# Accumulating transfers for the outer sums, early stored combinations, and two more third-level pairs in a Strassen-style kernel

## The chip, the cores and the metric

The kernel runs on one core of a Trainium2 chip. The metric is device time in microseconds for one execution. A core has five engines that run their own instruction streams in the order written: TensorE (PE, matrix products), VectorE (DVE), ScalarE (ACT), GpSimd (POOL) and SyncE (SP, which here only issues transfers). Transfers (DMA) between the memory outside (HBM) and the on-chip SBUF are issued by SP, by ACT or by POOL. PE writes its results to eight banks of PSUM, from which DVE or ACT take them.

## The reference

Two layers on x of shape (32, 128, 2048), all float32:

```python
# layer 0: a mixed 1x1 convolution, then a linear layer with 16 low-rank updates
out = einsum('boi,bih->boh', agg_w, x) + agg_b[:, :, None]
out = einsum('bsd,od->bso', out, W) + bias + sum_e w_e * (out @ A_e.T) @ Bf_e.T
x = x + out
# layer 1: a grouped convolution (9 taps) with a context term, then 16 heads of FFN
out = conv(x, weight, groups=4) + ctx + bias
t = out[:, perm].reshape(b * l, 16, 128)
t = gelu(t @ up[h]) @ down[h]            # per head, 128 -> 512 -> 128
x = x + t.reshape(...)[:, unperm]
```

The kernel folds the low-rank updates into W, multiplies x by that matrix (4096 rows by 2048 by 2048, the work that the change touches), and mixes the channels afterwards.

## The kernel before

**Outer level.** The large product is split in 2 by 2 blocks and computed by a scheme of seven products (Strassen-Winograd): `ROUNDS = P1, P2, P6, P7, P5, P3, P4`. Each round runs over eight groups g of rows, so there are 56 steps (r, g), in this order; below, P2/4 is round P2, group 4. A round needs a combination of the weight blocks (`outer_weights`, loaded and combined by POOL during the round before) and each step one of the x blocks (`x_loads`, `x_combine`, L285 to L318). The 2 by 2 blocks of the result are sums of these products. They are kept in memory: a step loads the old sum (`olds_load`, L1039, by the table `ADDED`, L323), adds to it, and stores it under a new name (`part_store`, on SP's queue). p1, u1, u2, u3 are intermediate sums, c00 to c11 the results; P5 loads and stores two.

**Inner levels.** In a step, `multiply` (L333) applies the seven products again: four matrix instructions of 512 columns each. `multiply_third` (L426) takes two consecutive steps (a pair, g even and g + 1) and replaces two of the seven products of each by a third level over both: the even step has five products, the odd step five products and seven "quarters" of 256 columns, into further banks. `THIRD` lists the rounds that do so, `SKIP` (L52) the pairs (round, g // 2) that don't. The sums of a pair are stored after its odd step. After each product, DVE adds its bank to the accumulator in SBUF (L342, L435, L458); only P1, which has no old sum, writes a block first by an ACT copy (L344). A product that continues a bank waits until the bank has been read.

**POOL.** In step i, ahead of its products, POOL combines x for step i + 1 (L283 and L311 to L314), makes the third level's inputs (`third_inputs`, L417 to L420, for even g over 0 except in P6) and weights (`third_weights`, L393 to L396, at g = 0), the next round's outer weights (`combine`, L522) and, at g = 7, its inner weights (`inner_weights`, L245). P6 stores one x combination, s2 (for P3), and one of the weights, t2 (for P4), both through POOL's queue.

**Order.** The program is written with a manual schedule: every engine, and so every queue of transfers, runs its instructions in the order in which the Python code emits them. Buffers are 24 slots of 1 MB; a load into a slot waits for what used it last. In the last round (P4) the steps of the second stage (mixing, convolution) come in between products, and after it the FFN (L813 to L840).

## Time and profile before

| what | value |
|---|---|
| time, median of 3 runs | 2601.73 us (2601.64 to 2603.4) |
| time of the profiled execution | 2603.33 us |
| its span in the profile | 2601.6 us |
| PE busy | 2582.1 us (99%) |
| DVE, POOL, ACT busy | 1476.3, 1322.5, 533.6 us |
| bytes moved | 608.28 MB, 234 GB/s on average |
| the seven rounds of the large product | 49.8 to 1478 us of the span |
| even step, odd step, step without a third level | 17.17, 29.25, 24.03 us (rounds P2 to P3) |

The steps' times come from the starts of PE's instructions, in order. In a row of a timeline the columns are the start and the length in us, engine, line, operation, what is written from what, how many are merged, and the idle time before it with its releaser. In a row of waits they are who waited for whom, then the total in us, how often, and the longest. In a row of stretches, each engine's busy time and number of instructions, the granted clock, the busy share of the transfer engines and what they moved in GB/s. A suffix q (SPq, ACTq) is the engine's instruction stream as an issuer of transfers.

### The profile page before, as it was taken

The page shows a single profiled execution, that of the slowest core. Times are in us where ns is not written, and L with a number is a line of the kernel's source. Part 1 is how long each engine was busy: PE and PEld are TensorE (multiplying, and loading weights), DVE is VectorE, ACT ScalarE, POOL GpSimd, SP SyncE. Part 2 cuts the span into 40 slices and gives each one's busy share as a digit, 9 for nine tenths or more (in the row PEclk, how much of TensorE's full clock was granted, in tenths as well). Part 3 has the DMA queues.
Part 4 walks back from the last instruction along what each step waited for, and adds up shares of the span by engine and source line. Part 5 has one row for each costly group of instructions (what it writes and reads, how often), then busy time and mean ns, then how long its engine had stood idle before and what let it go on. Part 6 is the DMA issues. An engine that isn't in the chain of part 4 may idle for free. (4 is left out here: it accounts for less than half of the span.)

```text
span 2601.6 us, 21348 instructions
## 1 busy us (share of the span) xinstructions
PE 2582.1 (99%) x6876; PEld 1304.0 (50%) x6876; DVE 1476.3 (57%) x2326; ACT 533.6 (21%) x1099; POOL 1322.5 (51%) x1092
## 2 busy tenths in 40 slices
PE   9999999999999999999999999999999999999998
PEld 4444455455455555555454544555545555455543
DVE  5554465356455676544276666667666666666610
ACT  0000000000000000000011244444444444444432
POOL 7321657888986854967323234343444334434232
PEclk9999999999999999999999999999999999999999
DMA  7542458688557487474767797877777877787532
GB/s 311 221 162 99 188 194 331 262 335 324 209 227 290 185 322 299 194 311 162 249 214 259 227 308 260 254 235 226 226 235 236 257 234 222 224 253 236 166 117 89
DMA packets 188160, 608.28 MB, mean 234 GB/s; under 512 B 17680, under 2 KB 92944, under 8 KB 144016
## 3 DMA queue, kind: packets, MB, share of 16 engines
q1 hardware_dynamic: 149936, 473.74, 51.3%
q0 software_dynamic: 32704, 130.04, 14.9%
q10 hardware_dynamic: 5408, 3.13, 0.4%
q8 instruction: 55, 0.90, 0.1%
q14 instruction: 57, 0.47, 0.1%
HBM read 372.45 MB, written 200.84 MB: 220 GB/s over the span
## 5 line engine op out<-in xcount | busy, mean ns | idle before, releaser
L818 PE MATMUL bank<-t,ws 128*128 128x512 f32 x1024 | 460.4, 592 | 0.0
L829 PE MATMUL bank<-gl,ws 128*128 128x512 f32 x1024 | 460.2, 592 | 0.0
L836 POOL DMA_INDIRECT out<-t,orow x128 | 151.0, 1180 | 543.8 <-DVE t L834 482.2
L821 ACT ACTIVATE gl<-bank 128x512 f32<-128x512 f32 x512 | 306.5, 599 | 445.2 <-PE bank L818 435.4
L829 PEld LDWEIGHTS bank<-gl,ws 128*128 128x128 f32 x1024 | 194.6, 190 | 233.0 <-issue 231.0
L818 PEld LDWEIGHTS bank<-t,ws 128*128 128x128 f32 x1024 | 194.5, 190 | 226.9 <-issue 223.0
L567 POOL TENSOR_TENSOR x<-x,fb 128x512 f32<-128x512 f32 x128 | 176.4, 1407 | 224.8 <-DMA x<-in_x 153.8
L834 DVE TENSOR_TENSOR t<-bank,t 128x512 f32<-128x512 f32 x128 | 88.5, 691 | 320.4 <-PE bank L829 320.4
L573 ACT ACTIVATE bank<-w,aggb 128x512 f32<-128x512 f32 x128 | 81.0, 684 | 872.9 <-DMA w<-w_d 855.6
L439 PE MATMUL bank<-P_t,s_P 128*128 128x512 f32 x544 | 241.8, 592 | 0.0
L435 DVE TENSOR_TENSOR u<-bank,u 128x512 f32<-128x512 f32 x168 | 110.7, 688 | 196.2 <-PE bank L439 178.1
L283 POOL TENSOR_TENSOR xt<-xt,xt 128x512 f32<-128x512 f32 x128 | 161.9, 1297 | 106.1 <-DMA xt<-in_xT 88.2
L311 POOL TENSOR_TENSOR s_P<-xt 128x512 f32<-128x512 f32 x56 | 73.3, 1308 | 254.9 <-DMA xt<-in_xT 185.2
L439 PE MATMUL bank<-wo_P,s_P 128*128 128x512 f32 x448 | 199.1, 592 | 0.0
L546 DVE SCALAR_TENSOR_TENSOR ags<-mix,att_bc,ags 128x128 f32<-128x128 f32 x224 | 184.8, 825 | 4.7
L439 PEld LDWEIGHTS bank<-P_t,s_P 128*128 128x128 f32 x544 | 103.4, 190 | 115.6 <-issue 112.4
L802 POOL DMA_INDIRECT t<-hx_d,row x128 | 131.8, 1030 | 53.1 <-issue 25.1
L349 PE MATMUL bank<-P_t,s_P 128*128 128x512 f32 x352 | 154.7, 592 | 0.0
L439 PEld LDWEIGHTS bank<-wo_P,s_P 128*128 128x128 f32 x448 | 85.1, 190 | 95.2 <-issue 92.6
L674 PE MATMUL bank<-va,tw_l 128*128 128x256 f32 x512 | 122.0, 380 | 1.0 <-DVE va L658 1.0
L342 DVE TENSOR_TENSOR u<-bank,u 128x512 f32<-128x512 f32 x84 | 56.4, 685 | 110.0 <-PE bank L349 108.6
L674 PEld LDWEIGHTS bank<-va,tw_l 128*128 128x128 f32 x512 | 96.8, 190 | 43.1 <-issue 32.4
(188 smaller groups left out, 3591.5 us busy)
## 6 DMA issues: line engine op xcount, KB each, us to landing
xt<-in_xT SPq DMA_DIRECT2D x88, 1024.0 KB
u<-u_d SPq DMA_DIRECT2D x40, 1024.0 KB
wo_P<-wb_d SPq DMA_DIRECT2D x36, 1024.0 KB
u<-c_d SPq DMA_DIRECT2D x64, 512.0 KB
x<-in_x SPq DMA_DIRECT2D x32, 1024.0 KB
xg<-x SPq DMA_DIRECT2D x256, 128.0 KB
hx_d<-x1t SPq DMA_DIRECT2D x32, 1024.0 KB
hx_d<-ht SPq DMA_DIRECT2D x32, 1024.0 KB
```

What stands on the lines that cost most here:

```text
L283: nc.gpsimd.tensor_tensor(out[:, i, j], a[:, i, j], b[:, i, j], op)
L349: nc.tensor.matmul(ps, lhsT=lhs[k][:, bass.ts(kc, P)], rhs=rhs[k][kc], start=first and kc == 0, stop=last and kc == 3, skip_group_check=True,)
L435: nc.vector.tensor_tensor(acc[:, si, oi], ps, acc[:, si, oi], ALU.add)
L439: nc.tensor.matmul(ps, lhsT=lhs[k][:, bass.ts(kc, P)], rhs=rhs[k][kc], start=first and kc == 0, stop=last and kc == 3, skip_group_check=True,)
L546: nc.vector.scalar_tensor_tensor(ag, mix[:, k], att, ag, ALU.mult, ALU.add)
L567: nc.gpsimd.tensor_tensor(xt[:, f], xt[:, f], late["fb"][:, f], ALU.add)
L674: nc.tensor.matmul(out, lhsT=w[:, 2 * i + r], rhs=rhs, start=first and r == 0, stop=last and r == 1, skip_group_check=True,)
L802: nc.gpsimd.indirect_dma_start(out=t.rearrange("p k t -> p (k t)"), out_offset=None, in_=hx_d[g].rearrange("l k t -> l (k t)"), in_offset= ...
L818: nc.tensor.matmul(pu, lhsT=w[:, m * P : (m + 1) * P], rhs=t[:, 0], start=True, stop=True)
L821: nc.scalar.activation(gl[m], pu, AF.Gelu)
L829: nc.tensor.matmul(pd, lhsT=w[:, (MC + m) * P : (MC + m + 1) * P], rhs=gl[m], start=(m == 0), stop=(m == MC - 1),)
L836: nc.gpsimd.indirect_dma_start(out=out, out_offset=bass.IndirectOffsetOnAxis(ap=orow[:, g, h : h + 1], axis=0), in_=t[:, 1], in_offset=None,)
```

## The change

1. `SKIP` loses (P2, 3) and (P5, 3): steps 6 and 7 of these rounds run as a pair with the third level.
2. The sums of outer products are no longer loaded and stored under new names. A table `SUMS` gives, for each round, what it loads, where it stores, and with what operation. P1 stores its product to c00 and c01. P2, P6, P5, P3 and P4 start a fresh accumulator and add it to the sums in memory by an accumulating transfer issued by POOL. P7 alone loads a sum (c01, which is then P1 + P6), adds to it and stores it to c11 and c10. The stores of a step are issued at its end (for a pair after the odd step). With a fresh accumulator the first write of each block is an ACT copy.
3. Combinations for later rounds are stored where they first arise: x(1,0) + x(1,1) for P5 in round P6 (s1), x(0,0) - x(1,0) for P7 in round P1 for g > 1 (s3; one more load, four POOL additions and a store on POOL's queue), and the weights of P7 at the combination for P6 (t3). P7 (g > 1) and P5 then load one x block, P7's weights one block for each kc.
4. s1, s2, t2 and t3 are stored through ACT's queue; s2 and t2 were on POOL's.

```diff
-SKIP = (("P2", 3), ("P6", 3), ("P5", 3))
+SKIP = (("P6", 3),)
...
-            "P7": lambda: [x_load(g, 0, 0), x_load(g, 1, 0)],
-            "P5": lambda: [x_load(g, 1, 0), x_load(g, 1, 1)],
+            "P7": lambda: [part_load("s3", g)] if g > 1 else [x_load(g, 0, 0), x_load(g, 1, 0)],
+            "P5": lambda: [part_load("s1", g)],
...
-            b, a, c = ts
-            pieces(b, b, a, ALU.add)
-            pieces(a, b, c, ALU.subtract)
-            part_store("s2", g, a)
-        if r in ("P7", "P5", "P3"):
-            pieces(a, a, ts[1], ALU.add if r == "P5" else ALU.subtract)
+            b, c, a = ts
+            pieces(b, b, c, ALU.add)
+            part_store("s1", g, b, nc.scalar)
+            pieces(a, b, a, ALU.subtract)
+            part_store("s2", g, a, nc.scalar)
+        elif len(ts) > 1:
+            pieces(a, a, ts[1], ALU.subtract)
...
+    SUMS = {
+        "P1": (None, ("c00", "c01"), None),
+        "P2": (None, ("c00",), ALU.add),
+        "P6": (None, ("c01",), ALU.add),
+        "P7": ("c01", ("c11", "c10"), None),
+        "P5": (None, ("c01", "c11"), ALU.add),
+        "P3": (None, ("c01",), ALU.add),
+        "P4": (None, ("c10",), ALU.add),
     }
+    def sum_store(r, g, acc):
+        for n in SUMS[r][1]:
+            if SUMS[r][2]:
+                nc.gpsimd.dma_start(
+                    part_d[n, g], acc.rearrange("p k s c -> p (k s c)"), accum_op=SUMS[r][2]
+                )
+            else:
+                part_store(n, g, acc, nc.sync)
+
+    def put(acc, fresh, si, oi, ps):
+        to = acc[:, si, oi]
+        if (si, oi) in fresh:
+            nc.vector.tensor_tensor(to, ps, to, ALU.add)
+        else:
+            nc.scalar.copy(to, ps)
+            fresh.update([(si, oi), (si, oi, 0), (si, oi, 1)])
+
+    def begin(r, g, old):
+        if old is not None:
+            return old, {(si, oi, *h) for si in range(2) for oi in range(2) for h in ((), (0,), (1,))}
+        return slot(f"m_{r}{g}", (P, 2, 2, QW)), set()
...
         def combine():
+            def keep(d, t):
+                nc.scalar.dma_start(d[kc], t.rearrange("p k o c -> p (k o c)"))
+
             if len(ts) > 1:
                 pieces(ts[0], ts[0], ts[1], ALU.subtract)
             if len(ts) > 2:
-                pieces(ts[0], ts[0], ts[2], ALU.add)
-                nc.gpsimd.dma_start(t2_d[kc], ts[0].rearrange("p k o c -> p (k o c)"))
-            return ts[0]
+                keep(t3_d, ts[0])
+                pieces(ts[2], ts[0], ts[2], ALU.add)
+                keep(t2_d, ts[2])
+            return ts[-1 if len(ts) > 2 else 0]
...
+    def sum_begin(i):
+        sums[i] = begin(*steps[i], olds.pop(i))
...
+        if ri == 0 and g > 1:
+            other = x_load(g, 1, 0)
         if in_pair(r, g):
...
+        if ri == 0 and g > 1:
+
+            pieces(other, xa[i], other, ALU.subtract)
+            part_store("s3", g, other)
         xa.pop(i - 1, None)
         if in_pair(r, g) and g % 2 == 0 and (g == 0 or r == "P6"):
             sq = third_inputs(i, nc.vector)
+        for what in stores:
+            sum_store(*what)
+        stores.clear()
```

More of the change, by code (lines that the diff above doesn't have):

```diff
@@ L104, in adaln_ffn_kernel @@
     t2_d = {kc: scratch(f"t2_d{kc}") for kc in range(4)}
+    t3_d = {kc: scratch(f"t3_d{kc}") for kc in range(4)}
     w1_d = scratch("w1_d", (1, L))
@@ L111, in adaln_ffn_kernel @@
         (n, g): scratch(f"{n}_d{g}")
-        for n in ("s2", "p1", "u1", "u2", "u3", "c00", "c01", "c10", "c11")
+        for n in ("s1", "s2", "s3", "c00", "c01", "c10", "c11")
         for g in range(NG)
@@ L320, in adaln_ffn_kernel, with multiply @@
     xa = {}
-    ADDED = {
-        "P1": [(None, "p1")],
-        "P2": [("p1", "c00")],
-        "P6": [("p1", "u1")],
-        "P7": [("u1", "u2")],
-        "P5": [("u1", "u3"), ("u2", "c11")],
-        "P4": [("u2", "c10")],
-        "P3": [("u3", "c01")],
-    }
-    def multiply(r, g, lhs, rhs, olds, between):
+    SUMS = {
[6 more added lines that the diff above has]
+        "P4": (None, ("c10",), ALU.add),
+    }
+    def sum_store(r, g, acc):
[17 more added lines that the diff above has]
+        return slot(f"m_{r}{g}", (P, 2, 2, QW)), set()
+    def multiply(r, g, lhs, rhs, acc, between):
         px, py, pz = bank(), bank(), bank()
-        accs = olds if olds[0] is not None else [slot(f"m_{r}{g}", (P, 2, 2, QW))]
-        fresh = set()
+        acc, fresh = acc
         def add(si, oi, ps):
-            for acc in accs:
-                to = acc[:, si, oi]
-                if olds[0] is not None or (si, oi) in fresh:
-                    nc.vector.tensor_tensor(to, ps, to, ALU.add)
-                else:
-                    nc.scalar.copy(to, ps)
-            fresh.add((si, oi))
+            put(acc, fresh, si, oi, ps)
         def product(k, ps, first, last):
@@ L376, in multiply @@
         done(px)
-        for (_, new), acc in zip(ADDED[r], accs):
-            part_store(new, g, acc, nc.sync)
+        stores.append((r, g, acc))
     def third_weights(name, rhs):
@@ L424, in third_inputs, with multiply_third @@
         }
-    def multiply_third(r, g, lhs, rhs, olds, between, quarters, sq):
+    def multiply_third(r, g, lhs, rhs, acc, between, quarters, sq):
         px, py = bank(), bank()
+        acc, fresh = acc
         if sq:
             qx, qy, qz = bank(), bank(), bank()
-            both = [held.pop(), olds]
+            both = [held.pop(), (acc, fresh)]
         def add(si, oi, ps):
-            for acc in olds:
-                nc.vector.tensor_tensor(acc[:, si, oi], ps, acc[:, si, oi], ALU.add)
+            put(acc, fresh, si, oi, ps)
         def product(k, ps, first, last):
@@ L455, in quarter @@
             for b, h in to:
-                for acc in both[b]:
-                    part = acc[:, :, 0, h * NQ : (h + 1) * NQ]
+                acc, fresh = both[b]
+                part = acc[:, :, 0, h * NQ : (h + 1) * NQ]
+                new = [si for si in range(2) if (si, 0, h) not in fresh]
+                if not new:
                     nc.vector.tensor_tensor(
@@ L460, in quarter @@
                     )
+                    continue
+                for si, p in enumerate(halves(ps)):
+                    if si in new:
+                        nc.scalar.copy(part[:, si], p)
+                        fresh.add((si, 0, h))
+                    else:
+                        nc.vector.tensor_tensor(part[:, si], p, part[:, si], ALU.add)
+                if {(1, 0, 0), (1, 0, 1)} <= fresh:
+                    fresh.add((1, 0))
         product("P1", px, True, False)
@@ L494, in multiply_third @@
         if not sq:
-            held.append(olds)
+            held.append((acc, fresh))
             return
-        for b, accs in enumerate(both):
-            for (_, new), acc in zip(ADDED[r], accs):
-                part_store(new, g - 1 + b, acc, nc.sync)
-    held = []
+        for b, (acc, _) in enumerate(both):
+            stores.append((r, g - 1 + b, acc))
+    held, stores = [], []
     def outer_weights(r, kc):
@@ L514, in outer_weights @@
             "P6": [w(1, 1), w(0, 1), w(0, 0)],
-            "P7": [w(1, 1), w(0, 1)],
+            "P7": [t3_d[kc]],
             "P5": [w(0, 1), w(0, 0)],
@@ L1033, in adaln_ffn_kernel @@
     unsummed, unsummed_first = [], list(first)
-    olds = {}
+    olds, sums = {}, {}
     chain = small()
@@ L1040, in olds_load @@
         r, g = steps[i]
-        olds[i] = [old and part_load(old, g) for old, _ in ADDED[r]]
+        olds[i] = SUMS[r][0] and part_load(SUMS[r][0], g)
+    def sum_begin(i):
+        sums[i] = begin(*steps[i], olds.pop(i))
     for i, (r, g) in enumerate(steps):
@@ L1045, in adaln_ffn_kernel @@
         last_round = ri + 1 == len(ROUNDS)
+        if i == 0:
+            olds_load(0)
+        sum_begin(i)
         if i + 1 < len(steps):
@@ L1054, in adaln_ffn_kernel @@
                     sq = third_inputs(i, nc.gpsimd)
-        if i == 0:
-            olds_load(0)
         if i + 1 < len(steps) and not last_round:
@@ L1127, in between @@
                     stage(k0 + j // 2, stage_second)
+        if ri == 0 and g > 1:
+            other = x_load(g, 1, 0)
         if in_pair(r, g):
             multiply_third(
-                r, g, lhs.pop(i), rhs, olds.pop(i), between, quarters, sq if g % 2 else None
+                r, g, lhs.pop(i), rhs, sums.pop(i), between, quarters, sq if g % 2 else None
             )
         else:
-            multiply(r, g, lhs.pop(i), rhs, olds.pop(i), between)
+            multiply(r, g, lhs.pop(i), rhs, sums.pop(i), between)
+        if ri == 0 and g > 1:
+            pieces(other, xa[i], other, ALU.subtract)
+            part_store("s3", g, other)
         xa.pop(i - 1, None)
```

## The prediction

> **What bounds the kernel now.** I read the page's engine table first, then what TensorE waited for, then the stretches of single steps.

> ```profile
> PE 2582.1 (99%) x6876; PEld 1304.0 (50%) x6876; DVE 1476.3 (57%) x2326; ACT 533.6 (21%) x1099; POOL 1322.5 (51%) x1092
> ...
> PE bank L223 <- DVE w L226: 3.2, 3, 2.5
> ...
> PE bank L450 <- POOL P_q L394: 1.4, 1, 1.4
> ```

> TensorE (PE) is busy 2582.1 of 2601.6 us and no single wait is over 2.5 us. So the time is PE's own work, and anything that makes PE stand is added in full. Adding up PE's gaps between 50 and 1478 us, the seven rounds, gives 4.6 us (1.44 of them in step P6/1, where the quarter weights of L394 come late). The change can remove only matmul time or these 4.6 us; earlier loads, fewer bytes and idler engines buy nothing.

> **Part 1: two more pairs with the third level.** The stretches show what a pair (two steps) takes with it and without it, in rounds P2 and P6:

> ```profile
> core 0: us, PE busy (x) PEld busy (x) DVE busy (x) ACT busy (x) POOL busy (x), PEclk, DMA share, GB/s
> 399.36:445.78 46.42, 46.42 (x137) 25.84 (x136) 24.08 (x35) 0.00 (x0) 32.98 (x28) 1.00 0.87 331
> 445.78:493.85 48.07, 48.07 (x114) 21.28 (x113) 14.44 (x23) 0.00 (x0) 36.79 (x32) 1.00 0.70 264
> ...
> 588.39:634.81 46.42, 46.42 (x137) 25.84 (x136) 30.14 (x39) 0.00 (x0) 38.31 (x32) 1.00 0.81 304
> 634.81:682.88 48.07, 48.07 (x114) 21.28 (x113) 18.11 (x23) 0.00 (x0) 44.27 (x37) 1.00 0.66 258
> ```

> 48.07 - 46.42 = 1.65 us a pair; (P2, 3) and (P5, 3) make **-3.3 us**, all of it on PE. With PE's 4.6 us of gaps, -7.9 us is the most that this change can bring.

> **Part 2: who issues the sums.** 48 loads of old sums leave SP's queue (56 become 8) and 32 of its 64 stores; 48 accumulating transfers come to POOL's queue, at the end of a plain step or of a pair. SP's relief is worth 0 by the above. On POOL the transfer's issue is short; the nearest row is POOL's own 1 MB store at 0.573 us (L277). The trace has no accumulating transfer: below I bound its issue by 0.57 and by 1.18 us, the indirect store of L836, and take 0.57. What counts is its wait. It must wait for the last DVE add of the step, and POOL does nothing behind it meanwhile, as POOL and SP do today in the like place:

> ```profile
> POOL out L836 <- DVE t L834: 482.2, 93, 10.1
> ...
> SPq L277 <- DVE u L458: 180.2, 12, 33.2
> ```

> The first row is POOL standing before a store until DVE has the data. Queued behind the new wait is POOL's next step: the combination of the next step's x, the third-level inputs (L417 to L420), the weights of the next round. Today POOL does these ahead. For step P2/4, which PE starts at 399.36:

> ```profile
> 387.65 1.26 POOL L311 TENSOR_TENSOR s_P<-xt 128x512 f32<-128x512 f32 x1 [5.78 <-DMA xt<-in_xT]
> ...
> 392.72 1.26 POOL L417 TENSOR_TENSOR sq<-xt 128x512 f32<-128x512 f32 x1
> ...
> 397.85 9.90 POOL L283 TENSOR_TENSOR wo_P<-wo_P,wo_P 128x512 f32<-128x512 f32 x8
> 408.04 0.57 POOL L527 DMA_DIRECT2D t_d<-wo_P  x1 [0.30 <-POOL wo_P L283]
> ```

> It began 11.7 us before the step and needs 20.1 us (387.65 to 407.75). After the change the step before it is the end of a pair: PE ends at E, the two last DVE adds take until E+1.5 (today 399.56 plus 1.29), then 0.1 and the issue of 0.57: POOL begins at E+2.15. By itself that is harmless: the result of the x combination is due at E+17 and is there at E+7.3.

> **Part 3: the early stores on ACT.** This is where it hurts. Six of the seven rounds now start their sums afresh, so the first write of each block of the accumulator is an ACT copy instead of a DVE add (0.587 us by the row L344 ACT COPY m_P, where a DVE add is 0.69; ACT has room). But ACT also receives the stores of combinations (s1, s2, t3, t2; 24 x 0.33 us by today's ACTq rows of L548, some 8 us), and these stand in ACT's stream **ahead of the copies of the running step**: x_combine(i+1) and combine() come before multiply(i) in the loop. Each store waits for POOL; every copy behind it waits too; and PE waits for the copy, because product P1's bank px is added into again by product P6:

> ```profile
> 399.36 3.60 PE L439 MATMUL bank<-w,xt 128*128 128x512 f32 x8
> 402.79 7.03 PE L439 MATMUL bank<-P_t,s_P 128*128 128x512 f32 x16
> 409.66 7.03 PE L439 MATMUL bank<-w,s_P 128*128 128x512 f32 x16
> ```

> These are the five products of an even step, 3.43 us each: P1 into px, P5 into py, then P6 into px. PE arrives at P6 6.87 us into the step. In an odd step the quarters lie between and it arrives at 3.43 + 3.45 + 3.43 + 3.45 = 13.8 us.

> Round P2, steps 4 and 6 (even, with a combine()): POOL has t2 at E+2.15+20.1 = E+22.25; 0.3 to ACT's issue (as before L527's), 0.33 for it, 0.69 for the copy with its hand-over: px is free at E+23.55. PE stands 23.55 - 6.87 = 16.7 us, twice: **+33.4 us**. Steps 3, 5 and 7 are odd: POOL has gone straight on from the even step (no sum is stored there), and its store comes about 11, 4 and 0 us into the step, before 13.8: nothing.

> Round P6, every x_combine stores s1 and s2, s2 after eight additions of 1.24 us (9.9 us by the 8-fold rows of L283). Steps 0, 2, 4 (even) and 6 (plain, behind a pair; PE reaches P6 after P1 and P2, also 6.87): E + 2.15 + 9.9 + 0.3 + 0.33 + 0.69 = 13.4, less 6.87 = 6.5 us, four times: **+26.0 us**. Odd steps: s2 comes some 4 us into them, nothing; P6/7 makes P7's x, which stores nothing. Behind these lies one unknown: the three x loads of a P6 step can land after E+2.15 (today POOL waited for them up to 5.3 us in this round). From 0 to 5 us each: I take 1, **+4 us**, since most of those loads were there. Step P6/1's own gap of 1.44 us goes, as its quarter weights get the time of the stall: **-1.4**.

> Rounds P7, P5, P3, P4 store nothing on ACT that waits for POOL. P5's four transfers put POOL at E+3.4, with 10.3 us of work due at E+17; P3: 10.2 us for the next x, then 10 more due at the odd step's quarters. P7 stores through SP as today. In P1 the added x load, four POOL subtractions (5 us) and the s3 store meet a POOL that idles 20 to 30 us a step; its loads compete for buffers: 0 to 10 us, taken as 0.

> DVE loses the second sum of P5, POOL 32 + 16 additions (P5's x, P7's weights, some 60 us): off the path, and hidden by PE. POOL's additions would only count in P6, where its 44.27 us in a plain pair of 48.07 are tightest, and there x keeps all its additions.

> [...] How long does an accumulating MB occupy queue and buffer? The row: POOL's plain stores landed in 9.4 us (s_d) to 10.0 us (t_d). [...] At today's 304 to 331 GB/s loads and stores clearly overlap; P5 loses 8 MB of plain old-sum traffic and two x loads per pair and gains four adds[...]. I take the row, and no loss from it.

> **The sum.** 33.4 + 26.0 + 4 - 3.3 - 1.4 = +58.7 us on a span of 2601.6. The profiled execution took 2603.3, the three timed runs have a median of 2601.7; the same addition to the median gives **2660 us**, +2.3%.

> **Rivals.**
> - No stall (6%): ACT's stores do not hold up its copies, or POOL isn't held at the pair's end. The point that decides: t2 issued before 6.2 us of step P2/4. For it: POOL is 12 us ahead today. Against it: 20 us of POOL work now stands behind a wait for the pair's end. Then 2601.7 - 3.3 = 2598 us, down to 2594 with all gaps gone: not slower.
> - Only P2 stalls (9%): in P6 POOL gets in ahead of the copies, say because the copies are due later than I read. 2601.7 + 33.4 - 3.3 = 2632 us.
> - The adds are slow (10%): accumulating transfers take over 40 us per MB, so that their buffers and the loads behind them come late and odd steps stall too, say 5 us in each of eight further pairs: 2700 us. For it: the DMA share is already 0.87 in a P2 pair. Against it: the bytes do not grow.

> **How the numbers follow.** The forecast has 75%; with buffer waits of P1, an issue of 1.18 instead of 0.57 (six stalls, up to two issues each: +7) and loads 0 to 5 us late in P6, it spans 2645 to 2685. To leave out no more than 2 in 10 the range takes in the second rival and the lower part of the third: 2632 to 2690. A change within 0.2%, 5.2 us, can't be told from none here: the first rival gives 4% same and 2% faster, the rest is slower, 94%.

> **What would show it.** Right: PE gaps of about 17 us in P2/4 and P2/6 and of 6 to 7 us in P6/0, 2, 4, 6, each ended by the ACT copy into the accumulator; ACT standing behind POOL's combinations; pairs P2/6-7 and P5/6-7 shorter by 1.65 us apart from gaps; SP's store waits shrunk. Wrong: PE still 99% busy, PE gaps ended by loads, or gaps in P5 and P3.

## The result, and the profile after

| | before | after |
|---|---|---|
| time, median | 2602.57 us (4 runs, 2601.64 to 2603.75) | 2707.12 us (4 runs, 2704.47 to 2709.5) |
| ratio, 95% interval | | 1.0401 [1.0389, 1.0414] |
| profiled span | 2601.6 us | 2707.7 us |
| bytes moved | 608.28 MB | 581.01 MB |

The changed kernel is 4.0% slower: +106.1 us of span, where +58.7 was forecast. Fewer bytes and fewer loads bought nothing, and TensorE (PE) is where the time went. The profile's engine row and its row of granted clock, in 40 slices of 67.7 us, read:

```profile
PE 2601.4 (96%) x6924; PEld 1321.3 (49%) x6924; DVE 1400.2 (52%) x2120; ACT 627.4 (23%) x1274; POOL 1315.0 (49%) x1094
...
PEclk9999898899899999999999989999999999999999
```

PE's share fell from 99 to 96%, and its busy time *rose* by 19.3 us with only 48 more matmuls. The second row says why: five slices show a clock below nine tenths (slices 5, 7, 8, 11 and 24 of 40), and each of them holds a stretch in which PE had stood. What it stood for, by the view of waits:

```profile
PE bank L457 <- ACT m_P L351: 51.8, 5, 16.8
PE bank L368 <- ACT m_P L351: 22.6, 2, 16.0
PE bank L850 <- DMA t<-hx_d,row: 10.7, 1, 10.7
PE bank L457 <- POOL s_P L313: 6.9, 1, 6.9
```

The matmuls of the three kinds of step are now L368, L457 and L468, the DVE add of `put` is L349, its ACT copy L351, the accumulating transfer L339, the FFN's gather L834. Seven gaps end with the ACT copy that frees a PSUM bank, one with a POOL instruction that ends beside such a copy, one with the FFN's first gather. In order of time: P1/7 16.02, P2/3 5.21, P2/4 16.80, P2/6 16.72, P6/0, 2, 4 and 6 6.44, 6.59, 6.88 and 6.60, the start of the FFN 10.65 us. Nothing stands in P7, P5 or P3.

Stretches show step P2/4, the odd step P2/5 behind it, P6/0, P1/7 and pair P5/6-7 (columns as in the stretches of before):

```profile
core 0: us, PE busy (x) PEld busy (x) DVE busy (x) ACT busy (x) POOL busy (x), PEclk, DMA share, GB/s
427.46:463.64 36.18, 19.38 (x42) 8.31 (x40) 9.78 (x11) 1.66 (x3) 34.16 (x28) 0.76 0.86 301
463.64:492.89 29.25, 29.25 (x97) 18.25 (x96) 8.46 (x17) 3.09 (x6) 2.26 (x3) 1.00 0.55 154
558.00:583.48 25.48, 19.04 (x41) 8.17 (x40) 16.15 (x7) 1.66 (x3) 23.38 (x22) 0.87 0.96 329
284.09:326.76 42.67, 26.65 (x57) 11.51 (x56) 10.32 (x14) 2.34 (x4) 28.60 (x25) 0.80 0.39 151
1106.00:1152.42 46.42, 46.42 (x137) 25.86 (x136) 15.22 (x20) 4.74 (x9) 43.38 (x36) 1.00 0.63 167
```

An even step takes 17.17 us undisturbed. P2/4 takes 36.18: 17.17, the gap of 16.80, and 2.21 more, in which PE ran the step's matmuls at half the clock. The odd step behind it is whole again. The last row is the gain: 46.42 instead of 48.07.

**Where 106 us went.** Each step's length, less its undisturbed length, less its gap, is taken as what the slow clock cost: 2.63 (P1/7), 2.64, 2.21, 1.96 (P2), 1.87, 1.72, 3.21, 2.41 (P6), together 18.65, and about 2.8 at the FFN's start (5.66 us of PE time at half clock).

| term | us |
|---|---|
| six gaps that the prediction placed (P2/4, P2/6, P6/0, 2, 4, 6) | +60.0 |
| gaps that it did not place: P1/7 16.0, FFN 10.7, P2/3 5.2 | +31.9 |
| half clock behind nine gaps, 18.65 + 2.8 | +21.5 |
| third level in two pairs | -3.3 |
| small gaps of before that are gone, by the steps' lengths (-1.4 was forecast) | -4.5 |
| the rounds begin later | +1.6 |
| sum (measured: +106.1; the FFN behind its gap is 1.1 shorter than before) | +107.2 |

**The foreseen mechanism** stands in four timelines of the changed kernel, DVE's, POOL's, ACT's and PE's, around step P2/4 (columns as before):

```profile
427.66 1.29 DVE L349 TENSOR_TENSOR m_P<-bank,m_P 128x512 f32<-128x512 f32 x2 [3.01 <-PE bank L457]
```

```profile
429.25 0.86 POOL L339 DMA_DIRECT2D c_d<-m_P  x1 [8.09 <-DVE ags L576]
429.82 1.57 POOL L313 TENSOR_TENSOR s_P<-xt 128x512 f32<-128x512 f32 x1
...
440.29 9.79 POOL L284 TENSOR_TENSOR wo_P<-wo_P,wo_P 128x512 f32<-128x512 f32 x8
```

```profile
445.24 5.20 ACTq L552 DMA_DIRECT2D t_d<-wo_P  x2
450.56 1.07 ACT L351 COPY m_P<-bank 128x512 f32<-128x512 f32 x2 [24.46 <-POOL wo_P L284]
```

```profile
427.46 3.60 PE L457 MATMUL bank<-w,xt 128*128 128x512 f32 x8
430.89 3.60 PE L457 MATMUL bank<-P_t,s_P 128*128 128x512 f32 x8
451.29 5.65 PE L457 MATMUL bank<-P_t,s_P 128*128 128x512 f32 x8 [16.80 <-ACT m_P L351]
```

The pair's last adds end at 428.95. POOL issued the sum 0.30 us later (its row names a short DVE instruction of the mixing, L576, that ends in between) and began the next step's work at 429.82, 2.36 us into P2/4, where before it was 11.7 us ahead of it. Its eight weight additions end at 450.08, ACT issues t2 (the second of two merged issues) and only then copies the banks, and PE has stood for 16.80 us. Its next eight matmuls took 5.65 us instead of 3.60: the half clock.

### The profile page after: what moved, and what is told of

The parts are those of the page before. It is cut to its first block, busy times and chain, and to the rows that moved or that the text cites. A ratio compares the mean times of both kernels' runs of the same rounds, so it can differ in the third digit from the quotient of the medians.

```text
span 2707.7 us, 21413 instructions
## 1 busy us (share of the span) xinstructions
PE 2601.4 (96%) x6924; PEld 1321.3 (49%) x6924; DVE 1400.2 (52%) x2120; ACT 627.4 (23%) x1274; POOL 1315.0 (49%) x1094
## 2 busy tenths in 40 slices
DMA packets 184415, 581.01 MB, mean 215 GB/s; under 512 B 17264, under 2 KB 92528, under 8 KB 143600
## 5 line engine op out<-in xcount | busy, mean ns | idle before, releaser
L850 PE MATMUL bank<-t,ws 128*128 128x512 f32 x1024 | 463.2, 595 | 10.7 <-DMA t<-hx_d,row 10.7
L351 ACT COPY m_P<-bank 128x512 f32<-128x512 f32 x177 | 102.8, 585 | 1198.8 <-PE bank L457 447.5
L457 PE MATMUL bank<-P_t,s_P 128*128 128x512 f32 x608 | 283.7, 615 | 58.6 <-ACT m_P L351 51.8
L349 DVE TENSOR_TENSOR m_P<-bank,m_P 128x512 f32<-128x512 f32 x129 | 87.8, 690 | 480.5 <-PE bank L457 228.9
L339 POOL DMA_DIRECT2D c_d<-m_P x48 | 42.0, 933 | 386.1 <-DVE m_P L478 160.5
L457 PEld LDWEIGHTS bank<-P_t,s_P 128*128 128x128 f32 x608 | 119.8, 198 | 196.9 <-issue 173.5
L457 PE MATMUL bank<-wo_P,s_P 128*128 128x512 f32 x480 | 213.3, 592 | 0.0
L578 DVE SCALAR_TENSOR_TENSOR ags<-mix,att_bc,ags 128x128 f32<-128x128 f32 x224 | 210.0, 938 | 5.5
L834 POOL DMA_INDIRECT t<-hx_d,row x128 | 132.3, 1034 | 48.0 <-issue 25.3
L368 PE MATMUL bank<-P_t,s_P 128*128 128x512 f32 x288 | 131.2, 610 | 22.6 <-ACT m_P L351 22.6
L457 PEld LDWEIGHTS bank<-wo_P,s_P 128*128 128x128 f32 x480 | 91.3, 190 | 102.2 <-issue 99.4
L313 POOL TENSOR_TENSOR s_P<-xt 128x512 f32<-128x512 f32 x42 | 57.6, 1371 | 168.8 <-DMA xt<-in_xT 140.0
L478 DVE TENSOR_TENSOR m_P<-bank,m_P 128x512 f32<-128x512 f32 x75 | 51.8, 690 | 156.4 <-PE bank L468 155.7
L284 POOL TENSOR_TENSOR xt<-xt,xt 128x512 f32<-128x512 f32 x96 | 125.8, 1451 | 0.0
## 6 DMA issues: line engine op xcount, KB each, us to landing
c_d<-m_P POOLq DMA_DIRECT2D x48, 1024.0 KB, 10.8
```

Of the source, the lines that this page charges most:

```text
L284: nc.gpsimd.tensor_tensor(out[:, i, j], a[:, i, j], b[:, i, j], op)
L368: nc.tensor.matmul(ps, lhsT=lhs[k][:, bass.ts(kc, P)], rhs=rhs[k][kc], start=first and kc == 0, stop=last and kc == 3, skip_group_check=True,)
L457: nc.tensor.matmul(ps, lhsT=lhs[k][:, bass.ts(kc, P)], rhs=rhs[k][kc], start=first and kc == 0, stop=last and kc == 3, skip_group_check=True,)
L578: nc.vector.scalar_tensor_tensor(ag, mix[:, k], att, ag, ALU.mult, ALU.add)
L834: nc.gpsimd.indirect_dma_start(out=t.rearrange("p k t -> p (k t)"), out_offset=None, in_=hx_d[g].rearrange("l k t -> l (k t)"), in_offset= ...
L850: nc.tensor.matmul(pu, lhsT=w[:, m * P : (m + 1) * P], rhs=t[:, 0], start=True, stop=True)
```

## The experiments

Every ratio is to the kernel before, timed beside it, with its 95% interval.

**1. Early stores on POOL's queue instead of ACT's.**

```diff
-            part_store("s1", g, b, nc.scalar)
+            part_store("s1", g, b)
...
-            part_store("s2", g, a, nc.scalar)
+            part_store("s2", g, a)
...
-                nc.scalar.dma_start(d[kc], t.rearrange("p k o c -> p (k o c)"))
+                nc.gpsimd.dma_start(d[kc], t.rearrange("p k o c -> p (k o c)"))
```

> The changed kernel with the four early stores (s1, s2, t3, t2) issued by POOL instead of ACT; nothing else. Theory A (the stores stand in ACT's stream ahead of the copies, and PE waits for the copies): the seven gaps of P2/3, P2/4, P2/6, P6/0, P6/2, P6/4 and P6/6 go, 65.2 us, and with them the half clock behind each, some 16 us: about 2626 us; the gaps of P1/7 (16 us) and at the start of the FFN (10.7 us) stay. Theory B (the accumulating transfers burden memory or buffers, and the copies only show it): the transfers are all still there, so the gaps stay and the time is within 15 us of 2707.

Measured: 2640.7 us, 1.015 [1.0133, 1.0167]. PE's waits in this kernel:

```profile
PE bank L368 <- ACT m_P L351: 16.0, 1, 16.0
PE bank L850 <- DMA t<-hx_d,row: 10.8, 1, 10.8
PE bank L457 <- POOL xt L284: 5.9, 1, 5.9
...
PE bank L457 <- POOL P_t L253: 2.1, 1, 2.1
...
PE bank L468 <- POOL P_q L412: 1.1, 1, 1.1
```

All seven gaps of P2 and P6 are gone, with the same accumulating transfers and the same bytes: the stores' place on ACT is their cause, not the memory. P1/7 and the FFN, where no ACT store stands ahead of the copy, are unmoved. Most of what is left over the expectation is new: gaps of 2.08 us in P6/0 and of 5.89 and 1.14 us in P6/1. There POOL has the last step's x with the third level's inputs and P6's outer weights (20 us), P6's first x (15 us) and its inner weights (21 us): 56 us in a pair of 46.4, begun late. In the changed kernel the stalls of P2 seem to have given it that time.

**2. First writes on DVE instead of ACT.**

```diff
-            nc.scalar.copy(to, ps)
+            nc.vector.tensor_copy(to, ps)
...
-                        nc.scalar.copy(part[:, si], p)
+                        nc.vector.tensor_copy(part[:, si], p)
```

> The changed kernel with the first writes of the accumulators as DVE copies instead of ACT copies; the early stores stay on ACT. Theory A: nothing that PE waits for stands behind ACT's stores any more, so P2 and P6 lose the same gaps as with the stores on POOL, about 2626 us, though a buffer that is still being stored (P1/7, perhaps P2/3) holds a DVE copy as it held an ACT copy. Theory B: 2690 us or more. A third possibility, that DVE is then too late for PE: gaps of 1 us or less in many steps, 2640 us.

Measured: 2696.43 us, 1.0368 [1.035, 1.0385]. The number is the one of theory B, but experiment 1 speaks against that theory, and the gaps did not stay where they were. They moved: P2/5 15.16, P2/7 10.49, P6's even steps and P6/6 3.2 to 4.2, P1/7 16.19, the FFN 20.06. In P2/5, ACT's queue and DVE show why:

```profile
452.02 5.20 ACTq L552 DMA_DIRECT2D t_d<-wo_P  x2
```

```profile
437.15 0.68 DVE L351 COPY m_P<-bank 128x512 f32<-128x512 f32 x1
459.97 0.69 DVE L351 COPY m_P<-bank 128x512 f32<-128x512 f32 x1 [22.14 <-issue]
```

The copy at 459.97 is the first write into a fresh accumulator. DVE stood for 22 us until then, though nothing is in front of the copy in its stream: by the reading that experiment 12 tests in P2/3, the accumulator takes the buffer of t3, whose store ACT issued only at 452.02 and whose last packet ended at 459.44. So a late store held a copy in two ways here, by its place in ACT's stream and by the buffer it reads, and the second followed the copy from ACT to DVE. P6's smaller gaps have another cause (last section). Why the FFN's gap doubled is left open.

**3. The accumulating transfers of P2 to P3 issued in the next step, behind POOL's work for it.**

```diff
+        for what in late_sums:
+            sum_store(*what)
+        late_sums.clear()
         if ri == 0 and g > 1:
             other = x_load(g, 1, 0)
...
-            sum_store(*what)
+            if last_round or not SUMS[what[0]][2]:
+                sum_store(*what)
+            else:
+                late_sums.append(what)
```

> The changed kernel with each accumulating transfer of rounds P2 to P3 issued one step later in POOL's stream, behind POOL's preparation for the next step and ahead of that step's products; the early stores stay on ACT. Theory A (POOL is held at the end of a pair, so that its preparation and the store behind it are late): POOL works ahead again, the gaps of P2/4, P2/6 and P6/0, 2, 4, 6 shrink from 60 us to under 10 us, about 2630 to 2640 us. If ACT's stores alone were enough to hold PE, without POOL being held: the gaps stay above 40 us, 2680 us or more.

Measured: 2675.68 us, 1.0287 [1.0269, 1.0304], between the two expectations. The gaps of P2/3, P2/4 and P6/2, 4, 6 are gone and P2/6's is 0.89: that POOL was held at the pair's end is the other half of the cause. But P2/5 now has 6.78, P6/0 21.12 and P6/1 7.46. At P6/0, POOL's timeline and ACT's:

```profile
542.82 4.92 POOL L284 TENSOR_TENSOR xt<-xt,xt 128x512 f32<-128x512 f32 x4 [7.40 <-DMA xt<-in_xT]
```

```profile
535.45 12.68 ACTq L278 DMA_DIRECT2D s_d<-xt  x2
548.23 1.07 ACT L351 COPY m_P<-bank 128x512 f32<-128x512 f32 x2 [29.91 <-POOL xt L284]
```

The x load lands late and POOL waits for it, s2 stands in ACT's queue for POOL, the copy behind s2. That the deferred sums kept the load's buffer is the likely reason; it was not isolated.

**4. The third level alone: the kernel before with one line of the change.**

```diff
-SKIP = (("P2", 3), ("P6", 3), ("P5", 3))
+SKIP = (("P6", 3),)
```

> The kernel before with the third level in the pairs (P2, 3) and (P5, 3) too, and nothing else of the change. If the gain of a pair is 1.65 us and buffers suffice: 3.3 us faster, 2598 us. If POOL or the buffers are too late at the ends of these rounds: the gain is lost to new gaps in P2/6, P2/7, P6/0, P5/7 or P3/0, 2600 us or more.

Measured: 2600.23 us (12 runs) against 2602.01 (15 runs), 0.9993 [0.9984, 1.0002]. P4/7 ends at 1473.88 instead of 1478.43 us, so the rounds are 4.55 us shorter, but the median gains only 1.8. None of the gaps that were feared in these rounds is there. Part of the gain is given back later, where the FFN waits 0.5 us for its weights; the rest is not explained. This is the best version of the study, not to be told from the kernel before.

**5. The FFN's first gathers issued ahead of the last accumulating transfers.**

```diff
+        if last_round and g == 7:
+            final = list(stores)
+            stores.clear()
         for what in stores:
...
             gather_two(0)
+            for what in final:
+                sum_store(*what)
```

> The changed kernel with one edit: in the last step the FFN's first two gathers are issued by POOL ahead of the last accumulating transfer. If that transfer's wait is what makes them late: the gap at the FFN's start goes, 10.7 us and some 3 us of half clock, 2693 to 2695 us. If the gathers wait for something else (the rows they read, the buffers): 2705 us or more.

Measured: 2697.2 us, 1.0369 [1.0352, 1.0387], 9.9 us less than the changed kernel. The gap of 10.65 is gone; 2.26 us for the FFN's weights come up behind it, by which the saving falls short. In the changed kernel POOL's timeline was

```profile
1573.10 0.88 POOL L339 DMA_DIRECT2D c_d<-m_P  x1 [21.63 <-ACT m_P L351]
1574.29 1.05 POOL L834 DMA_INDIRECT t<-hx_d,row  x1 [0.30 <-issue]
```

and in the kernel before

```profile
1460.49 1.01 POOL L802 DMA_INDIRECT t<-hx_d,row  x1 [4.71 <-DVE x L585]
```

There the first gather was issued 18 us before the last round ended, now 2 us after it.

**6. s3 left out at P1/6 and P1/7** (P7 loads two blocks there, as before).

```diff
-            "P7": lambda: [part_load("s3", g)] if g > 1 else [x_load(g, 0, 0), x_load(g, 1, 0)],
+            "P7": lambda: [part_load("s3", g)] if 1 < g < 6 else [x_load(g, 0, 0), x_load(g, 1, 0)],
...
-        if ri == 0 and g > 1:
+        if ri == 0 and 1 < g < 6:
```

> The changed kernel with one edit: s3 is stored in P1 for groups 2 to 5 only; P7 loads and combines two x blocks for groups 6 and 7. If P1/7's gap comes from its accumulator taking the buffer of s3 of group 6, whose subtraction POOL does only after the 21 us of inner weights: the gap goes, 16 us and 2.6 us of half clock, 2688 to 2690 us. If it is another buffer or POOL itself: the gap stays, 2705 us or more.

Measured: 2688.17 us, 1.0328 [1.0311, 1.0346]: 19 us less, and P1/7 has no gap. What s3 did there, POOL's timeline and ACT's in the changed kernel:

```profile
292.08 4.92 POOL L257 TENSOR_TENSOR w<-w 128x512 f32<-128x512 f32 x4
296.96 4.92 POOL L284 TENSOR_TENSOR xt<-xt,xt 128x512 f32<-128x512 f32 x4
302.18 0.55 POOL L278 DMA_DIRECT2D s_d<-xt  x1 [0.30 <-POOL xt L284]
```

```profile
306.50 0.58 ACT L351 COPY m_P<-bank 128x512 f32<-128x512 f32 x1 [21.63 <-DMA s_d<-xt]
```

The subtraction for s3 of P1/6 stands in POOL's stream behind 21 us of P2's inner weights (L253 to L257), its store behind the subtraction, and the accumulator of P1/7 takes the buffer that this store reads.

**7. Experiments 1, 5 and 6 together.** The edits are those shown there.

> The same without the later accumulating transfers: early stores on POOL, gathers first, s3 for groups 2 to 5. From the run with the stores on POOL alone (2641 us), less the P1/7 gap with its clock (18.8 us) and less the FFN's (10.8 us and about 3 of clock): 2608 us, with the gaps at the turn from P2 to P6 as they were (9 to 11 us and their clock). If delaying the sums is what frees POOL there, the run with all four edits is faster than this one.

Measured: 2609.55 us (8 runs), 1.0028 [1.0018, 1.0039]. Three causes removed take 97.6 of the 104.6 us away. PE's waits that are left in the rounds are POOL's, at P6/0 and P6/1:

```profile
PE bank L457 <- POOL xt L284: 4.2, 1, 4.2
...
PE bank L468 <- POOL P_q L412: 2.2, 1, 2.2
PE bank L457 <- POOL P_t L253: 2.1, 1, 2.1
```

**8. Experiments 3 and 7 together.** The edits are those shown there.

> The changed kernel with four edits together: early stores on POOL, accumulating transfers of P2 to P3 one step later in POOL's stream, the FFN's first two gathers ahead of the last accumulating transfers, and s3 stored for groups 2 to 5 only. If these are the causes: the gaps of P1/7 and of the FFN's start go too, and what is left is a late POOL at the turn from P2 to P6 (0 to 8 us): 2597 to 2612 us. If something else in the change costs time by itself (the transfers in memory, half-speed clock without gaps): above 2615 us.

Measured: 2621.05 us, 1.007 [1.0053, 1.0087], 11.5 us slower than without the late sums: P2/7 waits 5.35 us (its copy 17.14 for a buffer whose store was landing), P6/3 8.72 and P3/1 2.85 for DVE. POOL's lateness is cured, and buffers and DVE are late instead.

**9. Experiment 7, with POOL relieved:** the third inputs of P2/6-7 and four subtractions of P6's inner weights go to DVE, behind a step's products.

```diff
-            tt(t[:, 0, 1], t[:, 1, 1], t[:, 0, 1], ALU.subtract)
+            if name != "P6":
+                tt(t[:, 0, 1], t[:, 1, 1], t[:, 0, 1], ALU.subtract)
...
-        if in_pair(r, g) and g % 2 == 0 and (g == 0 or r == "P6"):
+        if in_pair(r, g) and g % 2 == 0 and (g == 0 or r == "P6" or (r, g) == ("P2", 6)):
             sq = third_inputs(i, nc.vector)
...
+            if r == "P2":
+                for a, b in zip(nxt["P7"], nxt["P3"]):
+                    nc.vector.tensor_tensor(a, b, a, ALU.subtract)
```

> The run with stores on POOL, gathers first and s3 for groups 2 to 5 (2609.6 us), with 10.2 us of POOL's work between P2/6 and P6/0 given to DVE: the third-level inputs of P2/6 and the four last subtractions of P6's inner weights, both behind the step's products. If POOL's lateness there (gaps of 2.1, 4.2 and 2.2 us and 4.5 us of half clock) is all that is left: 2597 to 2600 us, faster than the kernel before by the 3.3 us of the two pairs and its own small gaps. If DVE or another buffer then becomes late: 2603 us or more.

Measured: 2607.44 us (16 runs), 1.0019 [1.0012, 1.0027]: the expected win did not come. The waits for POOL in P6/0 and P6/1 are gone, and two new ones of 2.6 us come, each with some 3.4 us of PE at half clock behind it (from 441 to 488 us, around the first, the granted clock was 0.96):

```profile
PE bank L458 <- ACT m_P L352: 2.6, 1, 2.6
PE bank L469 <- DVE m_P L479: 2.6, 1, 2.6
```

The first is the buffer again (P2/7's copy waited 12.65 us for a store of s_d), the second DVE in P6/1, now busy with the moved work. Less these two waits (5.2 us) and half of the 6.8 us at half clock, about 2599 us would be left, an estimate. The third level alone gave 2600.23, so no large further cost of the accumulating transfers is hidden here.

**10. The early stores stay on ACT, but are issued behind the step's products.**

```diff
-            part_store("s1", g, b, nc.scalar)
+            early.append(lambda: part_store("s1", g, b, nc.scalar))
...
-            part_store("s2", g, a, nc.scalar)
+            early.append(lambda: part_store("s2", g, a, nc.scalar))
...
-                nc.scalar.dma_start(d[kc], t.rearrange("p k o c -> p (k o c)"))
+                early.append(
+                    lambda: nc.scalar.dma_start(d[kc], t.rearrange("p k o c -> p (k o c)"))
+                )
...
+        for what in early:
+            what()
+        early.clear()
         xa.pop(i - 1, None)
```

> The changed kernel with one edit: the early stores s1, s2, t3, t2 stay on ACT, but are issued behind the copies of the running step instead of ahead of them. If their place in ACT's stream is what holds PE: the seven gaps of P2 and P6 go, as with the stores on POOL, and 2626 to 2641 us remain (P1/7, the FFN's start and a late POOL at the turn from P2 to P6). If the stores' landing, in buffers that the fresh accumulators take, holds the copies: the gaps stay in part and may grow, since the stores start later: 2660 us or more.

Measured: 2650.18 us, 1.0183 [1.0168, 1.0199]. The gaps of P2/3, P2/6 and all four of P6 are gone, with ACT still the issuer: it is the order in ACT's stream that counts. New in P6 are a wait of 3.63 us for POOL at the start of P6/1 and waits of 1.4 us at most in the odd steps. P2/4 keeps 9.37 us, and ACT's row names the other way:

```profile
432.97 1.07 ACT L351 COPY m_P<-bank 128x512 f32<-128x512 f32 x2 [16.25 <-DMA c_d<-m_P]
```

The fresh accumulator waited for an earlier accumulating transfer out of its buffer, issued at 419.08 and landed at 432.87. The time lies between the two expectations, since both causes are at work.

**11. Experiments 9 and 10 together.** The edits are those shown there, with the early stores on ACT as in experiment 10.

> As the run before, but with the early stores on ACT behind the step's copies instead of on POOL, which spares POOL 24 issues of 0.57 us. If POOL is the tight engine at the turn from P2 to P6: as fast or faster than that run, 2596 to 2600 us. If a store that starts later keeps a buffer from the loads or accumulators behind it: slower than that run.

Measured: 2616.12 us, 1.0053 [1.004, 1.0067]. One gap of 9.59 us remains, in P2/4, and nothing else above 1.5. Its cause is that of experiment 10: the copy came at 414.71, when an accumulating transfer issued at 400.61 had landed at 414.61 (PE's row of waits names a POOL addition that ends beside the copy). So sparing POOL the stores did not help, and POOL remains the better place for them.

**12. No t3** (P7's weights from two loads, as before).

```diff
-            "P7": [t3_d[kc]],
+            "P7": [w(1, 1), w(0, 1)],
...
-                keep(t3_d, ts[0])
```

> The changed kernel without t3: P7's weights are loaded as two blocks and subtracted again, and combine() stores only t2 on ACT. In P2/3 the copies come 5.2 us after ACT has issued t2, with the landing of t3 as the releaser. If the fresh accumulator there waits for the buffer of t3 to be stored: the gap of P2/3 goes (5.2 us and 2.6 us of half clock), those of P2/4 and P2/6 stay at 16 to 17 us, and the time is about 2699 us. If ACT's place in the queue alone made that gap: it stays, since t2 is issued at the same time, and the time is within 2 us of 2707.

Measured: 2698.16 us, 1.037 [1.0352, 1.0387], 9 us less. P2/3's gap is gone and P2/4 (16.83) and P2/6 (16.73) stand as they were. ACT's rows of P2/3, in the changed kernel and then without t3:

```profile
398.29 5.38 ACTq L552 DMA_DIRECT2D t_d<-wo_P  x2
408.86 1.07 ACT L351 COPY m_P<-bank 128x512 f32<-128x512 f32 x2 [15.64 <-DMA t_d<-wo_P]
```

```profile
400.47 0.35 ACTq L552 DMA_DIRECT2D t_d<-wo_P  x1
400.92 1.07 ACT L351 COPY m_P<-bank 128x512 f32<-128x512 f32 x2 [10.58 <-POOL wo_P L284]
```

With t3 the issue of t2 was over at 403.67, yet the copy came at 408.86, just after t3 had landed (408.76); without t3 it comes 0.1 us behind t2.

## Why the prediction was wrong

The time lies 17 us above the range. The mechanism that the prediction put first was right, nearly to the digit. What failed is the sum, which put four terms at nothing or did not name them: the slow clock behind each gap (21.5 us), P1 (16.0), the odd steps of P2 (5.2), and the FFN's gathers behind the last transfer (10.7). They are 53.4 us together; the forecast was 47.4 us short, as the loads and the small gaps cost less than reckoned.

- **The third level** ("-3.3"): right, pairs P2/6-7 and P5/6-7 take 46.42 us apart from gaps.
- **POOL held at the pair's end** ("POOL begins at E+2.15"): right, E+2.36. The issue was taken as 0.57 us and measures 0.84 to 1.21, median 0.88, within the bounds of 0.57 to 1.18 but for the longest, and worth about 0.3 us a stall.
- **P2/4 and P2/6** ("16.7, twice"): right, 16.80 and 16.72. **P6/0, 2, 4, 6** ("6.5, four times"): right, 26.5 us together. The late x loads ("+4") did not show: 0.5 us. Experiments 1, 3 and 10 each undo one link of this chain. With the first all six gaps go. With the others all but one go or fall below 1 us, and that one stays for another reason.
- **The sum has no term for the clock.** This is the largest miss, 21.5 us; without it the time would lie at about 2686 us, inside the range. The trace of before has no gap over 1.44 us in the rounds and so could not show it. In the trace of the changed kernel each of the nine gaps, 5.21 to 16.80 us long, is followed by 3.0 to 6.0 us of PE time at a granted clock of 0.50, which cost 1.7 to 3.2 us a gap. Shorter gaps were followed by it too, two of 2.6 us in experiment 9 and one of 2.08 in experiment 7, while one of 2.08 in experiment 1 was not (last section).
- **"P1: 0 to 10 us, taken as 0"**: wrong, 16.0 us and beyond the bound. The reasoning took POOL's idle time per step, 20 to 30 us, as an average. P1/7 is the step in which POOL builds the next round's inner weights for 21 us, and s3's subtraction is queued behind them (experiment 6).
- **"Steps 3, 5 and 7 are odd: nothing"**: wrong for P2/3, 5.2 us. The store was in time, if only just: its issue was over 13.3 us into the step, where 11 was reckoned and 13.8 is the limit. The copy was held by its destination, the buffer of t3's store (experiment 12). The prediction followed the copy's place in ACT's stream and never asked which buffer a fresh accumulator takes. Before, the old sum's own load took the buffer well ahead of the step; now the first write takes it in the midst of it.
- **What is queued behind the transfer on POOL**: the prediction named "POOL's next step", and at the end of the last round that is the FFN's gathers: 10.7 us, and the clock (experiment 5).
- **An accumulating MB** ("I take the row", 9.4 to 10.0 us): near, as the row of the changed kernel shows:

```profile
c_d<-m_P POOLq DMA_DIRECT2D x48, 1024.0 KB, 10.8
```

It landed in 10.8 us, the median, against 9.4 (s_d) and 10.0 (t_d) for POOL's plain stores before: adding took hardly more. P5, with four per pair, shows no gap, so "no loss from it" held. The rival of slow adds names 2700 us, near the measured time, but not its cause: no step stalls for a slow add in P5, and experiment 7 has every add and 2609.55 us. Only in experiments 10 and 11 did a copy that held PE wait for an add to land, some 14 us from its issue.

Of the intentions of the change, then, 27 MB fewer bytes are worth nothing on this path, the third level 3.3 us of PE, and the accumulating transfers, the early stores on ACT and s3 each lay new work on an in-order stream that PE waits for. No variant with accumulating transfers was faster than the kernel before.

## What to carry to other kernels

In these traces a transfer issued from an engine's own stream held what stood behind it there until its data was ready (ACT's copy behind t2: PE stood 16.80 us in P2/4), so put it behind the work that others wait for. Where a buffer that was filled by an early load became one that is taken at its first write, that write inherited the wait of what was still being stored from the buffer (P2/3 5.21 us, P1/7 16.02): trace which store that is, for the busiest step and the last step too, not for the average one. Where a change leaves TensorE such gaps, reckon with slow clock behind them: it took 2.4 us a gap here (21.5 us for nine gaps of 5.2 to 16.8 us).

## What the runs showed that was not expected

**Long DVE instructions beside POOL's.** In the kernel before no DVE instruction of L578's kind (there L546) took over 1.7 us; in the changed one two of 224 took 10.5 and three 5.65. DVE's timeline and POOL's:

```profile
669.19 14.83 DVE L578 SCALAR_TENSOR_TENSOR ags<-mix,att_bc,ags 128x128 f32<-128x128 f32 x5
```

```profile
669.84 10.08 POOL L284 TENSOR_TENSOR xt<-xt,xt 128x512 f32<-128x512 f32 x8
```

One of the five took 10.50 us, from 669.58 until POOL's run of eight additions ended at 679.9. All five ended some 0.16 us after the last of POOL's additions that ran beside them back to back: eight of them beside those of 10.5 us, four beside those of 5.65. That POOL's additions held them is the author's reading of these times; no run isolates it. The likely reason that the change brings this about is that the same last adds release both engines: POOL through the transfer, DVE by ending. In the changed kernel it cost PE nothing, as no wait of PE in the rounds ends with a DVE add. In experiment 2 such a long DVE instruction stands ahead of P6's copies, here one of 8.77 us in P6/0, where a run of eight POOL additions ended at 555.06:

```profile
546.85 8.77 DVE L1144 TENSOR_TENSOR P_q<-P_t 128x512 f32<-128x512 f32 x1
555.54 0.68 DVE L351 COPY m_P<-bank 128x512 f32<-128x512 f32 x1
```

**The price of the clock hardly followed the length of the gap here, but where it fell.** In the trace of the changed kernel the gap of 16.72 us was followed by 3.48 us of PE time at half clock, that of 6.88 by 6.00, that of 6.59 by 2.99, and every change of the granted clock between 0.50 and 1.00 lies on one grid of 3.41 us. Experiments 1 and 7 have the same gap of 2.08 us in P6/0. In the stretches of two windows of such a grid in each, first of experiment 1, then of 7 (columns as in the stretches above), PE stood 1.72 us of the first window in the one and 2.08 us in the other, and only there the second window has half the clock:

```profile
516.38:519.79 3.41, 1.69 (x4) 0.39 (x3) 0.03 (x1) 0.00 (x0) 3.33 (x3) 1.00 0.00 0
519.79:523.20 3.41, 3.05 (x7) 1.44 (x8) 0.38 (x1) 0.59 (x1) 3.25 (x4) 1.00 0.00 0
```

```profile
497.89:501.30 3.41, 1.33 (x4) 0.68 (x4) 0.00 (x0) 0.00 (x1) 3.33 (x3) 1.00 0.00 0
501.30:504.71 3.41, 3.41 (x5) 1.35 (x4) 1.91 (x2) 0.58 (x1) 3.33 (x4) 0.50 0.00 0
```
